# State columns by DMA, three PSUM banks for one image, and a pool placed last, in a four-layer network

## The chip, the cores and the metric

The kernel runs on one core of a Trainium2 chip, as one program for a whole four-layer network. The metric is the device time of that program in microseconds, the median of several runs; lower is better. A core has five instruction streams that matter here: TensorE (PE, matrix products and transposes into the PSUM banks), VectorE (DVE), ScalarE (ACT), GpSimd (POOL), and SyncE (SP), which in this kernel does nothing but issue DMA transfers, in order, each after its own waits.

## The reference

Four images of 64 x 64 positions with 128 channels (`x` of shape (4, 64, 64, 128), float32) pass four layers. Each layer computes `x + L(gn(x))`, where `gn` is a group norm with 32 groups and `L` is what the comment names.

```python
# layer 0: selective scan over the 4096 positions, in 4 directions, 256 channels, 16 states
def step(h, xs):
    ut, dt, bt, ct = xs
    dA = jnp.exp(dt[..., None] * A)
    h = dA * h + (dt * ut)[..., None] * bt[:, :, None, :]
    y = jnp.einsum('bkdn,bkn->bkd', h, ct)
    return (h, y)
# layer 1: spectral mixing along both axes, then a two-layer feed-forward part and a layer norm
# layer 2: attention between channels (tokens), with spectral convolutions, then a mixer
# layer 3: attention of each position over its 7 x 7 neighbourhood, 4 heads:
#   q, k, v = qkv(x);  softmax(q k / sqrt(32) + rpb) v;  proj;  + x
```

The scan is the heart of layer 0: each of 256 channels x 16 states carries its own `h` along the sequence, for each image and each of the 4 directions, so `h` at the end of one piece of the sequence starts the next piece.

## The kernel before

**Layer 0.** The sequence of 4096 positions is cut into 8 chunks of 512 (`NCH`, `CH`). A unit is one image, one direction `k` and one chunk `c`: 4 x 4 x 8 = 128 units, run one after the other. A unit has 16 slots, one for each state index `n`. In a slot GpSimd forms `dB` from `du` and one row of `Bb` (L485, 128 x 1024); ScalarE forms `dA`, the exponential, for the two halves of the channels (L491, 128 x 512 each); VectorE runs two scans (L492) that write `h` and start from a column of `state`. TensorE transposes the `h` of an earlier slot (`pt`, L379, seven slots behind), ScalarE copies the result out of PSUM (`hT`, L389), and TensorE multiplies it with `W` (L414) to sum over the states. Four slots make a group `g`, with one `h` tile (three buffers), one `Bb` and one `W`, both loaded by DMA. The order on each of the four engines is the order in which the code is written (`manual_schedule`); SyncE's order is left to the tile scheduler.

Other work is threaded into the slots: the input parts of the next unit (`inputs`: `xd`, `Ct`, `delta`, `du`), and for other images the convolution ahead of the scan (`before`) and the norm and projection behind it (`after`). A function `later(place, f, ..., slots=m)` puts an instruction into a list for a place in a slot `m` slots on ("act1" is behind the second `dA` of that slot), and `flush` (L446) issues it there. Line 446 is therefore the line of all deferred instructions in the profile.

`state` is a tile of 128 x 2 x 16 numbers. At the end of each group (`q == 3`), for all chunks of a direction but the last, the last column of the four states is copied from `h` to `state`, where the next chunk's scans read it. Before the change it is an instruction of ScalarE:

```python
later("act1", nc.scalar.copy, state[:, :, 4 * g : 4 * g + 4], h[:, :, CH - 1, :], slots=5)
```

This happens 4 images x 4 directions x 7 chunks x 4 groups = 448 times.

**Layers 2 and 3.** On-chip arrays are held in pools, placed one behind the other, and a layer's pools are given up at its end; an array of the next layer that lies at an address of an old one waits for the old one's last use. Layer 2 (`layer2_image`, reached through a pacing helper, so nearly all of its instructions have L883) opens `l2big`, `l2tmp` and `l2small` in this order; its result is stored from an array of the pool `big` (`x<-m`, four stores an image). Layer 3 opens its weight pool `l3w` first (L1423), so in before it begins at the address of `l2big`.

In layer 3 a generator `front(b)` prepares image `b`. It loads `x`, then runs three stages over eight chunks of 512 positions: transposes `pg` (L1454), whose statistics VectorE takes (L1455) and which ScalarE copies to `xn` (L1456); products `pv`, to which VectorE adds the bias in `vt` (two buffers), stored to DRAM by two DMAs a chunk; products `pk` (L1482), which ScalarE copies with a bias to `kp` (L1485). `queries` then forms `pq` for a row of blocks and loads `V`. All of `pg`, `pv`, `pk` and `pq` are tiles of `psM`, which has one PSUM bank. For image 0 `front` runs alone before any attention; for images 1 to 3 its steps are threaded into the attention of the image before. The attention scores `ps3` are in `psS`: two buffers of two banks each.

Of the kernel before, what the change touches and what calls it, by code (L numbers as in the profile page):

```python
# [2 lines left out]

# [7 lines left out]
F32 = mybir.dt.float32  # L11
# [71 lines left out]
def layer0(sh, A, x_in, x_out, scr):  # L83
# [7 lines left out]
    with ExitStack() as ctx:  # L91
# [352 lines left out]
        def later(place, f, *a, slots=1, **kw):  # L444

            todo.setdefault((slot + slots, place), []).append(lambda: f(*a, **kw))  # L446
# [10 lines left out]
        with tc.manual_schedule(engines=order):  # L457
            for i, (b, k, c) in enumerate(units):
# [14 lines left out]
                for n in range(NS):  # L473
                    slot = NS * i + n
                    g, q = divmod(n, 4)
                    if q == 0:
                        B_now = Bb
                        if g < 3:
                            Bb = broadcast(bd, g + 1)
                        elif i + 1 < len(units):  # L480
                            Bb = broadcast(bd_next, 0)
                        h = tmp.tile([P, 2, CH, 4], F32, name="h", bufs=3)
                        G = dict(unit=unit, g=g, h=h, q=0)
                    dB = tmp.tile([P, 2, CH], F32, name="dB", bufs=3)
                    nc.gpsimd.tensor_tensor(dB, du, B_now[:, q : q + 1, :].to_broadcast([P, 2, CH]), ALU.mult)  # L485
                    flush("dve")
                    if i + 1 < len(units) and n in (9, 11):
                        next(coming)
                    for s in range(2):
                        dA = psx.tile([P, CH], F32, name="dA", tag="x")  # L490
                        nc.scalar.activation(dA, delta[:, s, :], AF.Exp, scale=A_neg[:, k, s, n : n + 1])  # L491
                        nc.vector.tensor_tensor_scan(  # L492
                            h[:, s, :, q], dA, dB[:, s, :], state[:, s, n : n + 1], ALU.mult, ALU.add
                        )
                        if s == 0 and i + 1 < len(units):
                            if n in (7, 8, 10):
                                next(coming)
                        elif n == 7 and i + 1 < len(units):
                            bd_next, Wd_next = next(coming)
                        flush(f"act{s}")  # L500
                    copy = transposed() if slot >= LAG else (lambda: None)
                    copy()
                    flush("act2")
                    if q == 2:
                        W = Ws[g] = tmp.tile([P, 32, 16], F32, name="W", bufs=4)
                        nc.sync.dma_start(W, Wd[g, 0 : P * CH].rearrange("(p t a) -> p t a", p=P, a=16))
                    if q == 3:
                        queue.append(G)
                        if c < NCH - 1:
                            later("act1", nc.scalar.copy, state[:, :, 4 * g : 4 * g + 4], h[:, :, CH - 1, :], slots=5)  # L510

                    if i + 1 < len(units):
                        if n == 1:
                            u_next, v_next = fetch(*units[i + 1])
                        if n == 6:
                            coming = inputs(*units[i + 1][1:], v_next, (i + 1) % 2)
                        if n in (6, 7, 9):
                            next(coming)
                        if n == 13:
                            ready = next(coming)  # L520

                    if n == 10:
                        y = unit["y"] = tmp.tile([P, 4, 2 * P], F32, name="y", tag="t4", bufs=4)
                        if k == 0:
                            src = scr("y3").rearrange("(w q r) d -> r w q d", w=64, r=2)
                            for r in range(2):
                                nc.sync.dma_start(y[64 * r : 64 * r + 64], src[r, :, 4 * c : 4 * c + 4, :])
                        elif k != 1:
                            nc.sync.dma_start(y, dst(1 if k == 3 else 0))

                    inside = [d for d in sides if d.inside]
                    free = n not in BUSY and not inside and slot >= taken
                    able = dict(f=False, l=False, m=free, n=free and n != 5, z=free and n != 5, c=free and n == 11)
                    for d in inside or [d for d in sides if able[d.need] and d.due(slot)][:1]:
                        taken = slot + dict(m=1, n=2, z=2, c=3)[d.need]
                        d.free_at = slot + 1
                        d.step()
                    for d in sides:
                        if d.need in ("f", "l") and d.due(slot):
                            if d.need == "l":  # L540
                                d.free_at = slot + 3
                            d.step()
                    sides = [d for d in sides if d.need]
# [833 lines left out]
def layer2(sh, w, wp, x_in, x_out, scr, wt):  # L1377
    tc, nc = sh.tc, sh.nc
    with ExitStack() as ctx:
        pool = lambda name, bufs, **kw: ctx.enter_context(tc.tile_pool(name=name, bufs=bufs, **kw))  # L1380
        ps = pool("l2ps", 3, space=PSUM)
        for name, shape in (("XG", [64, 5, P]), ("BD", [P, P])):
            w[name] = [wp.tile(shape, F32, name=f"{name}{n}") for n in range(2)]
            for t in w[name]:
                nc.vector.memset(t, 0.0)
        for t in w["XG"]:
            nc.vector.memset(t[:, 4, 64:65], 1.0)
        pools = pool("l2big", 1), pool("l2tmp", 1), pool("l2small", 1), ps
        paced = copy(sh)
        paced.nc = Pace(nc)  # L1390
        engines = {mybir.EngineType.PE, mybir.EngineType.Activation, mybir.EngineType.DVE, mybir.EngineType.Pool}
        free = [0, 1]
        pairs = [[] for _ in range(NB // 2)]

        def image(b):
            n = free.pop(0)
            yield from layer2_image(paced, w, pools, x_in(b), x_out(b), (scr(n), scr(2 + n)), wt, n, pairs[b // 2])
            free.append(n)

        with tc.manual_schedule(engines=engines):  # L1400
            paced.nc.in_turn((image(b) for b in range(NB)), 2)


def layer3(sh, A, x_in, out, v_pads):
# [5 lines left out]
    with ExitStack() as ctx:  # L1410
# [31 lines left out]

        def front(b):

            x = big.tile([P, NJ, DM], F32, name="x3")
            load_image(nc, x, x_in(b))
            xn = big.tile([P, NT], F32, name="xn3")
# [1 line left out]
            yield  # L1449
            st = small.tile([P, NCH, 6], F32, name="gn_st", bufs=2)  # L1450
            for c in range(NCH):
                pg = psM.tile([P, CH], F32, name="pg3", tag="m")
                for q in range(4):
                    nc.tensor.transpose(pg[:, q * P : (q + 1) * P], x[:, 4 * c + q, :], sh.ident)  # L1454
                nc.vector.bn_stats(st[:, c, :], pg)  # L1455
                nc.scalar.copy(xn[:, c * CH : (c + 1) * CH], pg)  # L1456
                yield
# [4 lines left out]
                nc.vector.tensor_scalar(xc, xc, s_, o_, ALU.mult, ALU.add)  # L1462
            yield
            for c in range(NCH):
                pv = psM.tile([P, 4, P], F32, name="pv3", tag="m")
                for q in range(4):
                    nc.tensor.matmul(
                        pv[:, q, :],
                        lhsT=xn[:, (4 * c + q) * P : (4 * c + q + 1) * P],
                        rhs=w["qkv"][:, 2 * P : 3 * P],  # L1470
                        start=True,
                        stop=True,
                    )
                vt = tmp.tile([P, 4, P], F32, name="vt")
                tt(vt, pv, w["v_b"].unsqueeze(1).to_broadcast([P, 4, P]), ALU.add)
                rows = v_pads[b % 2][3 + 8 * c : 11 + 8 * c, 3:67, :].rearrange("(q r) c d -> r c q d", r=2)
                for r in range(2):
                    nc.sync.dma_start(rows[r], vt[64 * r : 64 * r + 64])
                yield
            for c in range(NCH):  # L1480
                pk = psM.tile([P, CH], F32, name="pk3", tag="m")
                nc.tensor.matmul(  # L1482
                    pk, lhsT=w["qkv"][:, P : 2 * P], rhs=xn[:, c * CH : (c + 1) * CH], start=True, stop=True
                )
                nc.scalar.activation(  # L1485
                    kps[b % 2][:, 3 + 8 * c : 11 + 8 * c, 3:67],
                    pk.rearrange("p (h w) -> p h w", w=64),
                    AF.Identity,
                    bias=w["qkv_b"][:, 1:2],
                )  # L1490
                yield
# [343 lines left out]
```

## Time and profile before

The time is 8299.07 us, the median of 3 runs (8296.89 to 8299.89). The profiled execution has a span of 8299.4 us.

| engine | busy us | share of the span | instructions |
|---|---|---|---|
| PE matmul | 6571.5 | 79% | 52976 |
| DVE | 6753.8 | 81% | 7948 |
| ACT | 6229.0 | 75% | 10246 |
| POOL | 5482.7 | 66% | 2502 |
| DMA, SyncE's queue | | 44.0% of 16 engines | 1279618 packets |

Busy time doesn't include waits, and matmul ends are modelled. The shares are means over four layers with different limits: layer 0 ends at about 6006 us, layer 1 lies between that and about 6636, layer 2 goes on to 7692, and layer 3 takes the rest. A row of a group gives busy time, mean nanoseconds of one instruction and the idle time of its engine just before it, with what ended most of that. An arrow `a<-b` reads "a is made from b", and `[0.92 <-ACT dA L491]` in a timeline says that the engine stood idle 0.92 us until that instruction of another engine let it go.

### The profile page before, as it was taken

Reading aid. Unit: us, or ns where it says so; the run is one execution under the profiler, and the core shown is the slowest. Engines: PE = TensorE matmul, PEld = TensorE weight load, DVE = VectorE, ACT = ScalarE, POOL = GpSimd, SP = SyncE. Lnnn points to the kernel's source line nnn. Section 1 sums busy time; section 2 is a strip of 40 time slices with the busy share of each in tenths; the row PEclk is TensorE's granted clock in tenths of the full one; section 3 lists DMA queues with packets and bytes.
Section 4 is the critical chain, followed back from the end, with each engine's and each line's share of the span. In section 5 each row is a group of like instructions: output and inputs, shape, how many; then the busy total and the mean of one; then the engine's idle time right before and its main releaser. Section 6 shows DMA issues by size and latency. Waiting matters only on the chain.

```text
span 8299.4 us, 140501 instructions
## 1 busy us (share of the span) xinstructions
PE 6571.5 (79%) x52976; PEld 4171.0 (50%) x52976; DVE 6753.8 (81%) x7948; ACT 6229.0 (75%) x10246; POOL 5482.7 (66%) x2502
## 2 busy tenths in 40 slices
PE   7788888778788877888877777787779878686689
PEld 3444454444445444444544444454467766464456
DVE  2889999998999999889999999999944545645578
ACT  3899999989899898989988999999822213315467
POOL 0889889988888898888889999999800011020233
PEclk9899999999999999999999999999989988788799
DMA  6445555445555544455555445455442041331332
GB/s 127 153 143 188 162 164 176 158 156 166 176 168 172 173 165 161 157 169 168 176 179 170 157 156 185 174 174 181 148 103 43 23 118 35 87 101 31 96 94 79
DMA packets 1281977, 1163.78 MB, mean 140 GB/s; under 512 B 637973, under 2 KB 1075825, under 8 KB 1214354
## 3 DMA queue, kind: packets, MB, share of 16 engines
q1 hardware_dynamic: 1279618, 1153.06, 44.0%
q8 instruction: 417, 6.83, 0.3%
q14 instruction: 262, 2.15, 0.1%
q10 hardware_dynamic: 1680, 1.74, 0.1%
HBM read 962.66 MB, written 189.74 MB: 139 GB/s over the span
## 4 chain that ended last, share of the span: by engine, by line
PE 21%; ACT 11%; DVE 11%; issue 3%; DMA 2%; POOL 2%; SPq 1%; DVEq 0%; ACTq 0%; POOLq 0%
DVE h L492 4%; ACT hT L389 4%; ACT dA L491 4%; PE pt L379 2%; PE po L695 1%; PE pf L690 1%; POOL dB L485 1%; PE pz L883 1%; PE pu L883 1%; PE pt L1518 1%; DVE in_st L883 1%; PE pb L883 1%; DVE m L883 1%; PE pa L883 1%; PE ps L1572 1%
## 5 line engine op out<-in xcount | busy, mean ns | idle before, releaser
L492 DVE TENSOR_TENSOR_SCAN h<-dA,state,dB 128x512 f32<-128x512 f32 x4096 | 4958.8, 1269 | 361.5 <-ACT dA L491 247.2
L485 POOL TENSOR_TENSOR dB<-du,Bb 128x1024 f32<-128x1024 f32 x2048 | 4817.0, 2385 | 550.7 <-DVE h L492 381.9
L379 PE MATMUL pt<-ident,h 128*128 128x128 f32 x16384 | 2249.0, 281 | 1014.9 <-ACT hT L389 1010.0
L379 PEld LDWEIGHTS pt<-ident,h 128*128 128x128 f32 x16384 | 1838.5, 143 | 2051.6 <-ACT hT L389 1806.4
L491 ACT ACTIVATE dA<-delta,A_neg 128x512 f32<-128x512 f32 x4096 | 2746.1, 690 | 163.8 <-DVE h L492 140.8
L389 ACT COPY hT<-pt 128x1024 f32<-128x1024 f32 x2048 | 2068.3, 1010 | 176.9 <-PE pt L379 163.4
L414 PE MATMUL yT<-hT,W 128*32 128x256 f32 x16384 | 1396.9, 414 | 2.7 <-DVE y L430 2.1
L883 POOL COPY XG<-Xs 64x9 f32<-64x9 f32 (+2 forms) x44 | 10.9, 292 | 1020.8 <-ACT Xs L883 1020.7
L414 PEld LDWEIGHTS yT<-hT,W 128*32 128x32 f32 x16384 | 454.4, 150 | 352.0 <-issue 336.9
L214 PE MATMUL cv<-xn,taps 128*128 128x512 f32 x1152 | 612.8, 632 | 0.0
L1556 POOL TENSOR_TENSOR S<-S,sm 128x784 f32<-128x784 f32 x128 | 191.1, 1493 | 403.1 <-DVE sm L1554 251.9
L325 PE MATMUL dp<-xd,w_dt 65*128 65x512 f32 x512 | 298.1, 665 | 103.9 <-ACT Ct L312 91.8
L334 POOL TENSOR_TENSOR du<-delta,u 128x1024 f32<-128x1024 f32 x128 | 305.1, 2383 | 67.6 <-DVE delta L331 67.6
L214 PEld LDWEIGHTS cv<-xn,taps 128*128 128x128 f32 x1152 | 183.4, 188 | 234.0 <-issue 232.6
L306 PE MATMUL xd_ps<-u,w_x 128*48 128x512 f32 x512 | 251.8, 615 | 40.9 <-DMA u<-l_xw 16.8
L1563 ACT ACTIVATE S<-S,mx 128x196 f32<-128x196 f32 x512 | 227.9, 448 | 33.0 <-DVE mx L1590 32.4
L691 ACT ACTIVATE h<-pf,b 128x512 f32<-128x512 f32 x128 | 88.0, 687 | 146.7 <-PE pf L690 146.7
L331 DVE SCALAR_TENSOR_TENSOR delta<-delta,dp 128x512 f32<-128x512 f32 x256 | 169.2, 661 | 25.7 <-ACT delta L329 25.7
L325 PEld LDWEIGHTS dp<-xd,w_dt 65*128 65x128 f32 x512 | 79.4, 195 | 219.5 <-ACT Ct L312 150.4
L1432 POOL MEMSET kp<- 128x210 f32 (+1 forms) x8 | 1.8, 286 | 275.0 <-DMA x<-m 275.0
L328 ACT ACTIVATE delta<-dp 128x512 f32<-128x512 f32 x256 | 152.4, 595 | 28.4 <-PE dp L325 23.8
L329 ACT ACTIVATE delta<-delta 128x512 f32<-128x512 f32 x256 | 162.3, 634 | 8.1
(335 smaller groups left out, 7183.8 us busy)
## 6 DMA issues: line engine op xcount, KB each, us to landing
Bb<-l_B SPq DMA_DIRECT2D x512, 1024.0 KB
W<-l_W SPq DMA_DIRECT2D x512, 256.0 KB
l_y<-y SPq DMA_DIRECT2D x128, 512.0 KB
u<-l_xw SPq DMA_DIRECT2D x64, 512.0 KB
y<-l_y SPq DMA_DIRECT2D x64, 512.0 KB
u<-l_xr SPq DMA_DIRECT2D x64, 512.0 KB
V<-l_v SPq DMA_DIRECT2D x512, 49.0 KB
wr<-wt SPq DMA_DIRECT2D x128, 136.0 KB
```

The lines of the kernel that those rows point to most:

```text
L214: nc.tensor.matmul(pm, lhsT=taps[:, s, t, :], rhs=xn[:, dy : dy + 8, dx : dx + 64], start=(t == 0), stop=(t == 8),)
L306: nc.tensor.matmul(xd_ps, lhsT=w_x[:, s, k, :], rhs=u[:, s, :], start=(s == 0), stop=(s == 1))
L325: nc.tensor.matmul(dp, lhsT=w_dt[:, k, s * P : (s + 1) * P], rhs=xd, start=True, stop=True)
L334: nc.gpsimd.tensor_tensor(du, delta, u, ALU.mult)
L379: nc.tensor.transpose(pt[:, j, s, :], G["h"][:, s, t0 : t0 + 32, :].rearrange("p t n -> p (t n)"), sh.ident)
L389: return lambda: nc.scalar.copy(hT, pt.rearrange("p j s d -> p j (s d)"))
L414: nc.tensor.matmul(U["yT"][e][32 * jo : 32 * jo + 32, qo % 2, :], lhsT=U["Ws"][G["g"]][:, :, 4 * q + j], rhs=hT[:, j, :], start=((e, jo) n ...
L485: nc.gpsimd.tensor_tensor(dB, du, B_now[:, q : q + 1, :].to_broadcast([P, 2, CH]), ALU.mult)
L491: nc.scalar.activation(dA, delta[:, s, :], AF.Exp, scale=A_neg[:, k, s, n : n + 1])
L492: nc.vector.tensor_tensor_scan(h[:, s, :, q], dA, dB[:, s, :], state[:, s, n : n + 1], ALU.mult, ALU.add)
L883: r = f(*args, **kw)
L1563: nc.scalar.activation(Sn, Sn, AF.Exp, bias=U["mx"][:, n : n + 1], accum_out=sm[:, n : n + 1])
```

## The change

Three edits. The state columns go from `h` to `state` by a DMA that SyncE issues, written at the end of the group itself and not five slots later. The pool `l2big` is opened after `l2tmp` and `l2small`, so that layer 3's first arrays lie where these two were and not where the arrays are from which layer 2 stores its last result. And for image 0 of layer 3 `front` takes its PSUM tiles in turn from `psM` and from the two buffers of the scores, three banks in all. Lines of the changed kernel are one to ten higher than those of before.

```diff
-                            later("act1", nc.scalar.copy, state[:, :, 4 * g : 4 * g + 4], h[:, :, CH - 1, :], slots=5)
+                            nc.sync.dma_start(state[:, :, 4 * g : 4 * g + 4], h[:, :, CH - 1, :])
...
-        pools = pool("l2big", 1), pool("l2tmp", 1), pool("l2small", 1), ps
+        tmp, small, big = pool("l2tmp", 1), pool("l2small", 1), pool("l2big", 1)
+        pools = big, tmp, small, ps
...
         def front(b):
 
+            ring = itertools.count()
+
+            def bank(name):
+                if b == 0 and next(ring) % 3:
+                    return psS.tile([P, 2, CH], F32, name="ps3")[:, 0, :]
+                return psM.tile([P, CH], F32, name=name, tag="m")
...
-                pg = psM.tile([P, CH], F32, name="pg3", tag="m")
+                pg = bank("pg3")
...
-                pv = psM.tile([P, 4, P], F32, name="pv3", tag="m")
+                pv = bank("pv3").rearrange("p (q d) -> p q d", q=4)
...
-                pk = psM.tile([P, CH], F32, name="pk3", tag="m")
+                pk = bank("pk3")
```

More of the change, by code (lines that the diff above doesn't have):

```diff
@@ L1 @@
+import itertools
 from contextlib import ExitStack
```

## The prediction

> **What bounds the kernel now.** I read the page first: busy time, slices and dearest groups.
>
> ```profile
> DVE  2889999998999999889999999999944545645578
> PEclk9899999999999999999999999999989988788799
> L492 DVE TENSOR_TENSOR_SCAN h<-dA,state,dB 128x512 f32<-128x512 f32 x4096 | 4958.8, 1269 | 361.5 <-ACT dA L491 247.2
> ```
>
> A slice is 207 us. VectorE is at 80 to 90% through the first three quarters, layer 0, and one group, the scan, does three fifths of the span. The clock row falls only in the last quarter.
>
> Second, the busy time of each engine between 216 and 6006 us, layer 0's steady loop (columns: length; busy PE, PE weight load, DVE, ACT, POOL; clock; DMA share; GB/s), and VectorE's largest waits there (sum, count, longest):
>
> ```profile
> 216.00:6006.00 5790.00, 4606.56 (x36113) 2729.94 (x36114) 5401.90 (x5127) 5265.52 (x7879) 5183.43 (x2252) 0.98 0.51 167
> DVE h L492 <- ACT dA L491: 247.2, 406, 1.9
> DVE h L492 <- POOL dB L485: 90.9, 51, 4.9
> ```
>
> DVE, ACT and POOL are busy 93, 91 and 90%. They are near balance, so relieving one of them is worth only the part of its work on which the others wait. VectorE stands still 5790 - 5402 = 388 us (about 372 us in the scan's slots), 247 of it for ScalarE's `dA`.
>
> Third, the state copies, as their own row of groups by shape and once in the timeline (columns: start, length):
>
> ```profile
> L446 ACT COPY state<-h 128x8 f32<-128x8 f32 x448 | 82.6, 184 | 0.0
> ```
> ```profile
> 2507.45 0.18 ACT L446 COPY state<-h 128x8 f32<-128x8 f32 x1
> 2507.54 0.63 ACT L446 ACTIVATE e<-e 128x512 f32<-128x512 f32 x1
> 2508.07 0.99 ACT L389 COPY hT<-pt 128x1024 f32<-128x1024 f32 x1
> 2508.96 0.70 ACT L491 ACTIVATE dA<-delta,A_neg 128x512 f32<-128x512 f32 x1
> 2509.76 2.46 DVE L492 TENSOR_TENSOR_SCAN h<-dA,state,dB 128x512 f32<-128x512 f32 x2 [0.92 <-ACT dA L491]
> ```
>
> The copy never waits (0.0 in the last column); it only takes room. Here it stands in an unbroken ScalarE chain at whose end VectorE had stood 0.92 us: in such a slot its 0.18 us is on the path.
>
> Fourth, the seam of layers 2 and 3, where image 0's `front` runs alone. Timeline, then windows:
>
> ```profile
> 7692.36 0.35 SPq L1423 DMA_DIRECT2D qkv<-in_qkv_w  x1
> 7699.87 10.21 SPq L720 DMA_DIRECT2D x<-x  x8
> 7704.34 1.09 PE L1454 MATMUL pg<-ident,x 128*128 128x128 f32 x4 [32.63 <-DMA x<-x]
> 7705.53 0.70 DVE L1455 BATCH_NORM_STATS2 gn_st<-pg 128x6 f32<-128x512 f32 x1 [10.48 <-PE pg L1454]
> 7706.31 0.58 ACT L1456 COPY xn<-pg 128x512 f32<-128x512 f32 x1 [20.42 <-DVE gn_st L1455]
> 7706.95 1.12 PE L1454 MATMUL pg<-ident,x 128*128 128x128 f32 x4 [1.52 <-ACT xn L1456]
> ```
> ```profile
> 7704.34:7724.60 20.26, 8.89 (x32) 5.69 (x32) 5.96 (x9) 4.68 (x8) 0.00 (x0) 0.50 0.55 166
> 7728.70:7751.60 22.90, 16.58 (x64) 14.26 (x64) 6.70 (x9) 0.00 (x0) 0.00 (x0) 0.50 0.36 94
> 7751.60:7774.50 22.90, 16.61 (x17) 4.02 (x17) 0.00 (x0) 5.55 (x8) 0.00 (x0) 0.50 0.25 70
> 6813.20:6823.50 10.30, 10.24 (x31) 4.90 (x31) 0.00 (x0) 5.47 (x8) 0.00 (x0) 0.76 0.78 182
> 6644.50:6651.70 7.20, 5.43 (x32) 4.85 (x32) 5.19 (x9) 0.00 (x0) 0.00 (x0) 0.79 1.15 290
> ```
>
> PE, DVE and ACT go strictly in turn, since the next `pg` needs the bank that the ACT copy has just read; PE runs at half clock. The three windows are `pg`, `pv` and `pk`, 66 us with almost nothing beside them. The last two windows are layer 2's likenesses of `pk` and `pg`, with several banks: 10.3 against 22.9 us, and 7.2 against 20.3.
>
> **What the Trainium skill says.** "PSUM — Partial Sum Buffer", section "PSUM bank collisions raise a hardware error": two engines must not be on one bank at once, readers included. The trace agrees: ACT's `xn` copy, which needs only `pg`, starts after the statistics end. "TensorE: Matmul & The Clock Gate", section "Part 1: The HAM clock gate": the array starts at half rate and warms only when kept busy for some microseconds. The trace agrees: 0.50 through the front, 0.76 where layer 2 keeps PE busy. "DMA: Bandwidth & Descriptors", section "Anatomy of one DMA — SWDGE (gpsimd) path": about 2 us fixed for a transfer, mostly the receipt; here the first 512 KB of `x` took about 4.4 us, so I take 2 to 4 us for 4 KB of states; no row of before shows one. Its section "Why small descriptors are slow (HBM only)" says that small packets between SBUF and SBUF don't suffer as those of HBM do; no run so far shows one.
>
> **Part 1, states by DMA.** 448 copies leave ScalarE (4 images x 4 directions x 7 chunks x 4 groups), 448 x 0.184 = 82.6 us. Not all is on the path. Taking each copy in the trace, in 185 cases ScalarE ran without a gap from the copy to a wait of VectorE (90 in slot 8 of 16, 50 in slot 4, 23 in slot 12, 22 elsewhere); in the other 263 ScalarE idled first, as it does most in slot 6. That is 185 x 0.184 = 34 us. I take 28, as a slot won here is partly lost at the next wait for GpSimd (91 us of those remain). Ends: 0, if the next wait takes it all; 82.6, if ScalarE were the bound throughout.
>
> What it adds: SyncE issues 448 transfers. The nearest row, the `Ct` writes with their many small pieces, takes a median of 0.36 us: 160 us of issue over 5790, on a queue that has these waits alone:
>
> ```profile
> SPq L340 <- POOL dB L485: 1960.7, 324, 14.0
> ```
>
> So the issue is hidden. The added wait is SyncE's, for the last scan of a group. Behind it queue `Bb`, `W`, `u` and the next unit's small loads. In the changed order each `Bb` load that follows a state transfer belongs to a group at least three groups on and waits for GpSimd anyway; the tightest, the next unit's second group, is left about 17 us, against 2 to 4 for a state plus about 6 for a 1 MB `Bb`. Whoever reads the state is the next chunk's scan, 12 slots or more away: 12 x 2.83 = 34 us. `h` is reused 8 slots (22.6 us) after its end; today the copy comes only 5 slots after. Packets: 448 x 256 = 114,688 of 16 bytes. At the mean of all of before (44% x 16 x 8299 / 1,279,618 = 46 ns) they take 5.2 ms, 328 us of each of 16 engines, 0.51 to 0.57 of the loop at most: no bound. Part 1: -28.
>
> **Part 2, pool order.** With the arrays placed last, layer 3's weights no longer wait for layer 2's last `x<-m` stores. In the changed order fourteen loads stand before these stores, so layer 3's `x` goes at about 7692.4 instead of 7699.87: -7.5. The weights wait for `tmp`'s last use instead, near 7624, hidden under the last layer-2 image. At layer 2's start the `xg` loads go directly behind the last store, ahead of `wr`, whose issue held them from 6636.51 to 6639.10: -2.6.
>
> **Part 3, three banks.** `pg`: layer 2's likeness needed 12.6 us from the issue of the load to the end of its statistics; here it was 7724.6 - 7692.4 = 32.2 less a little, 31.6 with the same end marks. So 31.6 - 12.5 = -19.1, which includes the 7.5 above. `pv`: eight steps of 2.86 us. The PE time, 16.6, stays at half clock; `vt` has two buffers, so step n waits for the landing of n-2: addition 0.69, two issues 1.24, about 2 landing, some 4 us for two steps at best. With V stores between, I take 2.3 a step, 18.5: -4.4 (ends 16.6 and 19.2). `pk`: 22.9 to 10.3 as in layer 2 if the clock warms: I take 12, -10.9; the cold end is 16.6, -6.3. The first `pq`: -0.5. Images 1 to 3 keep one bank and run under attention, where PE is full: 0. Sum of the seam: -19.1 - 4.4 - 10.9 - 0.5 = -34.9.
>
> **Sum.** -28 - 2.6 - 34.9 = -65.5: 8299.1 - 65.5 = 8233.6, say 8233.
>
> **The rivals.** *A: the sum*, 8233. *B: layer 0 gains nothing.* For it: POOL is busy 90% and scans wait 91 us for it; against it: 185 copies stand right before a wait for `dA`. Seam alone, -38: 8261. *C: slower.* The state transfers hold up what is queued behind them on SyncE, or small pieces slow the big loads. For it: DMA share is 0.51, and `Bb` and `W` are in the same queue; against it: `Bb` has 17 us. At 0.25 us of stall for each of 448, +112, less 38 at the two seams and 28 in the scans: 8299 + 112 - 66 = 8345 (8373 without the 28). *D: ScalarE is the bound throughout.* For it: 247 of 388 us idle wait on it; against it: it idles 114 us in slot 6. -82.6 - 38: 8178.
>
> **How the numbers follow.** A 0.66, B 0.17, C 0.08, D 0.07, and 0.02 for a seam worth only 20 with layer 0 as it is (8279). Range 8195 to 8270: the low end is 60 us from scans with a seam of 44 at its best; the high end is B with a cold `pk` and slow `pv`. Faster by over 0.2% (16.6 us) is A, B, D and most of the last: 0.90; within, 0.03; slower, C's 0.07.
>
> **What would show it.** Right: no `state<-h` on ScalarE, 448 more issues on SyncE's queue; in the loop ScalarE about 83 less, VectorE's wait for `dA` 25 to 35 less, no scan waiting on a DMA; the loop's end some 28 us earlier; the `x` of layer 3 issued within a microsecond of the last store; `pg` about 8 us, `pk` at 1.3 to 2 a step. Wrong: scans waiting on DMA `state` or `dB` waiting on DMA `Bb` for more than the copy's 0.18 (then C), or `dA` waits that fall while waits on `dB` rise by as much (B), or `pv` held by its stores at 2.9 a step.

## The result and the profile after

The changed kernel took 8235.44 us (median of four runs; 8233.59 to 8247.49) against 8299.48 us before (also four): a ratio of 0.9925, with a 95% interval of 0.9908 to 0.9943. The profiled executions, 8299.4 and 8232.3 us, can be split at the same points. "First S" is the first addition of the bias to the scores in layer 3.

| stretch | before | after | difference |
|---|---|---|---|
| start to first scan | 225.5 | 225.6 | +0.1 |
| first to last scan (layer 0's loop) | 5781.2 | 5755.1 | -26.1 |
| last scan to layer 2's first `pg` | 637.8 | 634.7 | -3.1 |
| from there to layer 2's last store issued | 1044.9 | 1046.2 | +1.3 |
| to the issue of layer 3's `x` | 10.4 | 3.0 | -7.4 |
| issue of `x` to first S | 79.2 | 43.4 | -35.8 |
| first S to the end | 520.4 | 524.3 | +3.9 |

First the page of the changed kernel: slices, the scan's group, and SyncE's DMA queue (packets, MB, share of 16 engines).

```profile
DVE  2889999998999999889999999999944554635778
PEclk9899999999999999999999999999989989798799
L493 DVE TENSOR_TENSOR_SCAN h<-dA,state,dB 128x512 f32<-128x512 f32 x4096 | 4960.2, 1271 | 340.3 <-ACT dA L492 211.7
q1 hardware_dynamic: 1401474, 1154.93, 45.5%
```

The scan is as busy as before (4960 us); what shrank is the idle time ahead of it, 361.5 to 340.3, most of it in waits for `dA`, so the gain is mainly in ScalarE's lateness. Next, the busy time in the loop (same columns as before), VectorE's waits and SyncE's:

```profile
216.00:5980.00 5764.00, 4600.03 (x36114) 2727.96 (x36115) 5400.60 (x5127) 5228.49 (x7431) 5183.04 (x2252) 0.98 0.52 168
```
```profile
DVE h L493 <- ACT dA L492: 211.7, 366, 2.1
DVE h L493 <- POOL dB L486: 85.7, 48, 4.9
DVE h L493 <- issue: 18.1, 40, 1.4
DVE h L493 <- DMA W<-l_W: 7.4, 5, 1.5
```
```profile
SPq L511 <- DVE h L493: 1109.8, 290, 11.5
SPq L341 <- POOL dB L486: 1096.1, 273, 12.8
```

ScalarE has 448 instructions fewer, but its busy time in the loop fell by 37.0 us (5265.5 to 5228.5), not by the 83 that the prediction gave as a sign: 37.0 / 448 = 0.083 us a copy. The reason is that ScalarE's instructions overlap in the trace. The timeline in the prediction shows it: the copy starts at 2507.45 and is recorded as 0.18 us long, but the next instruction starts at 2507.54, only 0.09 us later. The median of all 448 copies in before is 0.088 us from start to next start.

SyncE's waits mostly changed their name: where it stood 1960.7 us for `dB`, it now stands 1109.8 us for the end of a group and 1096.1 us for `dB`. Scans wait 85.7 us for `dB`, not more than the 90.9 of before, so `Bb` isn't late. VectorE's waits for `dA` changed their names too. "Issue" rose from 5.4 to 18.1 us, and five waits stand under the load of `W`, which a scan doesn't read. In these five, and in 37 of the 40 under "issue", the scan started 0.09 us after its `dA` had ended, so they are waits for `dA`. Counted that way (waits over 0.15 us whose scan starts within 0.13 us of the end of its `dA`), before has 251.2 us and after 235.2. The waits for `dA` fell by 16.0 us, not by the 35.5 that the names suggest, and the trace shows no scan that waited for a DMA.

The transfer itself, from the view of its line (duration min/median/max in ns):

```profile
L511 SPq DMA_DIRECT2D state<-h x448: 599/600/1944, 235.1 to 5935.0; - x150
```

From the start of its issue to the end of its last packet such a transfer took 2.05 us (median, worked out from the packets).

Then the seam: SyncE's queue and the engines in the timeline, and the stages by window (`pg`; group scale; `pv`; `pk` to first scores).

```profile
7664.63 9.96 SPq L721 DMA_DIRECT2D x<-x  x8
7668.81 1.08 PE L1463 MATMUL pg<-ident,x 128*128 128x128 f32 x4 [24.96 <-DMA x<-x]
...
7683.34 2.76 SPq L1487 DMA_DIRECT2D l_v<-vt  x4
7686.44 1.70 SPq L1520 DMA_DIRECT2D V<-l_v  x2
7688.24 2.62 SPq L1487 DMA_DIRECT2D l_v<-vt  x4
...
7692.65 0.69 DVE L1484 TENSOR_TENSOR vt<-pv,v_b 128x512 f32<-128x512 f32 x1 [3.95 <-DMA l_v<-vt]
...
7707.11 1.58 PE L1581 MATMUL ps<-kp,q 32*64 32x196 f32 x32 [0.87 <-ACT q L1509]
```
```profile
7668.81:7676.22 7.41, 6.45 (x32) 5.50 (x32) 5.41 (x8) 4.10 (x7) 0.00 (x0) 0.68 1.15 347
7676.22:7680.51 4.29, 0.94 (x5) 0.80 (x5) 2.64 (x8) 0.85 (x2) 0.00 (x0) 0.59 0.61 185
7680.51:7694.71 14.20, 9.91 (x64) 9.34 (x65) 5.32 (x7) 0.00 (x0) 0.00 (x0) 0.86 0.35 90
7694.71:7707.11 12.40, 10.75 (x20) 3.93 (x19) 1.38 (x2) 6.38 (x10) 0.00 (x0) 0.75 0.45 120
```

`pg` takes 7.4 us where it took 20.3, and the clock column, 0.50 throughout before, is 0.86 in `pv`. What now holds `pv` stands in the last column of the `vt` line: VectorE waits for the store of an earlier `vt`, and the stores share SyncE's queue with the first `V` loads, whose issue holds the queue for 1.6 to 1.7 us at a time. Before, VectorE waited at `vt` for the products alone. Its waits there, before and after:

```profile
DVE vt L1475 <- PE pv L1467: 16.2, 8, 2.2
```
```profile
DVE vt L1484 <- DMA l_v<-vt: 9.6, 5, 3.9
```

### The profile page after: what moved, and what is told of

It is laid out like the page before. It is cut to its first block, busy times and chain, and to the rows that moved or that the text cites. A ratio compares the mean times of both kernels' runs of the same rounds, so it can differ in the third digit from the quotient of the medians.

```text
span 8232.3 us, 141196 instructions
## 1 busy us (share of the span) xinstructions
PE 6551.1 (80%) x52976; PEld 4166.6 (51%) x52976; DVE 6752.2 (82%) x7948; ACT 6192.0 (75%) x9798; POOL 5481.8 (67%) x2502
## 3 DMA queue, kind: packets, MB, share of 16 engines
q1 hardware_dynamic: 1401474, 1154.93, 45.5%
## 4 chain that ended last, share of the span: by engine, by line
PE 21%; DVE 11%; ACT 10%; issue 3%; DMA 2%; POOL 2%; SPq 1%; ACTq 0%; DVEq 0%; POOLq 0%
DVE h L493 5%; ACT hT L390 4%; ACT dA L492 3%; PE pt L380 2%; POOL dB L486 1%; PE po L696 1%; PE pf L691 1%; PE pz L884 1%; PE pt L1527 1%; PE pu L884 1%; DVE in_st L884 1%; PE pb L884 1%; DVE m L884 1%; PE pa L884 1%; PE ps L1581 1%
## 5 line engine op out<-in xcount | busy, mean ns | idle before, releaser
L493 DVE TENSOR_TENSOR_SCAN h<-dA,state,dB 128x512 f32<-128x512 f32 x4096 | 4960.2, 1271 | 340.3 <-ACT dA L492 211.7
L884 POOL COPY XG<-Xs 64x9 f32<-64x9 f32 (+2 forms) x44 | 10.9, 293 | 1016.6 <-ACT Xs L884 1016.5
L1527 PE MATMUL pt<-ident,S 128*98 128x128 f32 x1024 | 165.3, 286 | 3.3 <-POOL S L1565 1.9
```

What stands on the lines that cost most here:

```text
L493: nc.vector.tensor_tensor_scan(h[:, s, :, q], dA, dB[:, s, :], state[:, s, n : n + 1], ALU.mult, ALU.add)
L884: r = f(*args, **kw)
L1527: nc.tensor.transpose(pt[:, half, hp, :], U["S"][:, e, hp, 98 * half : 98 * half + 98], sh.ident)
```

## The experiments

**Each part alone.** `states_only` is before with the one line of the transfer; `pools_only` and `banks_only` are before with the other two edits one at a time; `seams_only` has both and ScalarE's copies:

```diff
-                            nc.sync.dma_start(state[:, :, 4 * g : 4 * g + 4], h[:, :, CH - 1, :])
+                            later("act1", nc.scalar.copy, state[:, :, 4 * g : 4 * g + 4], h[:, :, CH - 1, :], slots=5)
```

> Before, with the state columns by DMA alone. Theory 1 (the parts are independent, the scan loop gains what the changed kernel's loop gained): the last scan ends about 26 us earlier, time 8299 - 26 = 8273, all of it in layer 0. Rival (part of the loop's gain in the changed kernel was chance, or the transfers cost more than they look): within 10 us of before.

> The changed kernel with ScalarE's deferred copies put back: pool order and three banks alone. Theory 1: layer 0 as before (within 5 us), the start of layer 2 about 2 us shorter, the seam before layer 3 about 42 us shorter, of which up to 4 may be lost again in the attention by a lower granted clock: 8299 - 41 = 8258. Rival: the attention gives nothing back, 8255 or less.

> Before, with the pool order alone. Theory 1: weights are loaded ahead of the last stores, so x of layer 3 is issued about 7.5 us earlier, and layer 2 starts 2 us earlier: -9.5, 8290; the stages pg, pv and pk keep their 20, 23 and 23 us. Rival (the earlier load only meets the same wait for the bank or for the last store): no gain, 8297 to 8301.

> Before, with the three banks alone. Theory 1: x comes as late as before, the three stages shrink from about 70 us to about 38: -32, 8267. Rival (the stages gain only together with the earlier loads, because pg is then bound by the arrival of x): -20, 8279.

| kernel | median us | ratio to before | loop us | last store to `x` | `x` to first S | first S to end |
|---|---|---|---|---|---|---|
| states_only | 8282.38 | 0.9975 (0.9966 to 0.9985) | 5748.2 | 10.2 | 79.1 | 526.0 |
| seams_only | 8258.90 | 0.9946 (0.9929 to 0.9962) | 5787.3 | 3.0 | 43.3 | 525.0 |
| pools_only | 8292.85 | 0.9988 (0.9981 to 0.9995) | 5770.9 | 3.0 | 78.8 | 523.7 |
| banks_only | 8273.64 | 0.9964 (0.9951 to 0.9977) | 5783.2 | 10.6 | 43.0 | 528.9 |

Within these intervals the parts are independent: pool order (0.12%) and banks (0.36%) agree with the 0.54% of both, and with the states' 0.25% with the 0.75% of the whole. In the stretches of the table each edit shows at its own place. The time from the last scan to layer 2's last store, which the table leaves out, is 1682.7 us in before, 1674.7 in pools_only and 1692.9 in states_only, so single profiles don't add up as the medians do. Two more numbers are less exact than they look. The loop of kernels with the same layer 0 differs by up to 16 us (5770.9 to 5787.3; mean with before 5780.7). And the attention takes 520.4 us in before and 523.7 to 528.9 in the four others, with pools_only among them, so the +3.9 of the table isn't something that three banks cause.

**Is it the engine or the place?** ScalarE keeps the copies, in other slots:

```diff
-                            nc.sync.dma_start(state[:, :, 4 * g : 4 * g + 4], h[:, :, CH - 1, :])
+                            later("act1", nc.scalar.copy, state[:, :, 4 * g : 4 * g + 4], h[:, :, CH - 1, :], slots=(3, 5, 2, 2)[g])
```

> The changed kernel with the state copies on ScalarE again, but put 3, 5, 2 and 2 slots after the ends of the four groups (slots 6, 12, 13 and 1 of a unit, where ScalarE has the most idle time) in place of 5 each (slots 8, 12, 0, 4). Theory 1 (a copy costs only where VectorE then waits for a late dA; the changed kernel won half of its loop gain in slot 10, behind the copy of slot 8): the loop wins 13 to 26 of the 29 us without any DMA, about 8240. Rival 1 (ScalarE is in order and each copy costs the same wherever it stands): as with the two seams alone, 8258. Rival 2 (two or three slots after a group ScalarE must wait for the group's last scan, and is then late for the next dA): slower than 8258.

8231.18 us, ratio 0.9914 (0.9900 to 0.9928): as much as by DMA. ScalarE does all of its copies, as the row of groups says,

```profile
L447 ACT COPY state<-h 128x8 f32<-128x8 f32 x448 | 83.3, 186 | 0.0
```

and they cost next to nothing. Then only the first group's copy was moved, `slots=(3, 5, 5, 5)[g]`:

> The changed kernel with the state copies on ScalarE, of which only the first group's is moved, from slot 8 to slot 6; the other three stay 5 slots after their groups. Theory 1 (half of the loop's gain is in slot 10, behind the copy of slot 8): VectorE's idle time in slot 10 falls from 49 to about 38 us and the loop wins 12 to 15 us over the two seams alone, 8244. Rival (the gain is spread over the four copies evenly): a quarter, 7 us, 8251, with slot 10 hardly changed.

8248.99 us, ratio 0.9926 (0.9914 to 0.9939), 0.20% below the two seams alone, though the two intervals overlap; the loop is 5765.0, 16 us below the mean of 5780.7. One copy of four seems to carry half of the gain or more; as loops with one layer 0 differ by 16 us, one trace can't say it more exactly.

**What does the transfer cost?** None at all (then every chunk starts from the zero state, so the carried part of the scan is left out), and two instead of one:

```diff
-                        if c < NCH - 1:
-                            nc.sync.dma_start(state[:, :, 4 * g : 4 * g + 4], h[:, :, CH - 1, :])
```
```diff
+                            nc.sync.dma_start(spare_state[:, :, 4 * g : 4 * g + 4], h[:, :, CH - 1, :])
```

> The changed kernel without any copy of the state columns: every chunk's scans start from the zero state, so the carried part of the scan is left out; the work of each engine is else the same. Theory 1 (the transfers are hidden): as the changed kernel, 8235, within 5 us. Rival (the transfers cost on SyncE's queue or in the DMA engines): faster than the changed kernel by more than 10 us, 8225 or less.

> The changed kernel with a second transfer of each state column, to a spare tile: 448 more transfers of 256 pieces. Theory 1 (SyncE and the DMA engines have room): as the changed kernel, 8235, within 5 us. Rival (each transfer costs): slower by what a transfer costs times 448; 0.05 us each would give 22 us, 8257.

8234.72 us (0.9914, 0.9900 to 0.9927) without and 8229.24 us (0.9906, 0.9891 to 0.9921) with twice as many, against 8235.44. The transfers are hidden; no cost can be measured. VectorE's waits of the kernel without copies, in the same window as above, bear this out:

```profile
DVE h L493 <- ACT dA L492: 222.5, 397, 1.9
DVE h L493 <- POOL dB L486: 92.0, 50, 4.9
DVE h L493 <- issue: 3.5, 5, 1.4
```

318.0 us in sum, against 211.7 + 85.7 + 18.1 + 7.4 = 322.9 with the transfers.

**Two copies on ScalarE** (the two seams, and behind each copy a second one, to a spare tile):

> The changed kernel with ScalarE's deferred copies put back and a second copy of each column, to a spare tile, right behind. Theory 1 (about a third of a copy's 0.18 us is on the path, as in the removal): 448 x 0.065 = 29 us more than the two seams alone, 8287. Rival 1 (ScalarE bounds the loop throughout): 83 more, 8341. Rival 2 (the room is used up slowly, the removed copies were only late ones): within 8 us of 8258.

8300.06 us, ratio 0.9994 (0.9986 to 1.0002), 0.48% or 40 us over the two seams alone; in the profile the loop is 5823.1, 42 us over the mean of 5780.7. So 448 copies more cost 42 us (0.094 us each), and 448 fewer won 26 (0.058 each): dearer than expected when added. ScalarE's busy time in the whole run rose by 41.1 us (6229.9 to 6271.0), so the added copies cost about all the time that they took of ScalarE; the 83 us of their recorded lengths were never there to lose. That ScalarE isn't the bound throughout is shown by the copies in other slots: there it is as busy (6227.0 us), and the loop is 25 us shorter than with the two seams alone (5762.6 against 5787.3).

The next table is worked out from the traces: VectorE's idle time in two of the 16 slots, summed over all units, and how many of 128 units have a slot 10 of over 4 us (start of its first scan to the start of the next slot's; mean 4.5 to 4.8, against about 3.2 in the others).

```
                 loop us   idle in slot 4   idle in slot 10   units with a long slot 10
copies_twice     5823.1    47.2             71.6              28
seams_only       5787.3    41.9             49.3              15
before           5781.2    41.1             47.0              14
copy0_placed     5765.0    42.5             39.0              12
copies_placed    5762.6    37.7             38.1              11
after            5755.1    37.2             36.7               8
states_none      5749.7    36.7             27.5               4
states_twice     5745.1    37.2             29.3               4
```

Moving the first group's copy changes slot 10 and leaves slot 4 (42.5); moving the others mends slot 4. What a copy costs in a typical unit is seen in the median length of slot 10: 3.425 us with two copies ahead of it (copies_twice), 3.340 with one (before) and 3.257 with none (after), 0.08 us for each. Part of slot 10's cost comes in lumps: a unit is either short or 1.2 to 1.6 us longer. One long case, in the kernel with two copies, in the timeline and by windows:

```profile
2265.79 2.08 PE L326 MATMUL dp<-xd,w_dt 65*128 65x512 f32 x2
2267.90 0.60 ACT L329 ACTIVATE delta<-dp 128x512 f32<-128x512 f32 x1 [1.42 <-PE dp L326]
2268.53 0.63 ACT L330 ACTIVATE delta<-delta 128x512 f32<-128x512 f32 x1
2269.07 0.68 ACT L493 ACTIVATE dA<-delta,A_neg 128x512 f32<-128x512 f32 x1
2269.78 1.29 DVE L494 TENSOR_TENSOR_SCAN h<-dA,state,dB 128x512 f32<-128x512 f32 x1 [1.76 <-ACT dA L493]
```
```profile
2260.00:2263.75 3.75, 1.97 (x18) 1.08 (x17) 2.90 (x3) 3.72 (x9) 2.38 (x1) 1.00 0.76 54
2263.75:2268.00 4.25, 4.25 (x20) 2.14 (x21) 4.25 (x5) 2.83 (x5) 3.40 (x2) 0.63 0.88 212
```

Read upwards: the scan waits for `dA`, this stood in line behind the two activations of `delta`, these waited for `dp`, and `dp` took 2.08 us at a clock of 0.63, after a stretch in which TensorE was busy 1.97 of 3.75 us. In all long units of five traces (before, after, seams_only, states_none, copies_twice) `dp` took 1.4 to 2.1 us; its mean in the short ones is 1.13 to 1.16. In the record of the granted clock, which in the loop is either 1 or 0.5, `dp` met the 0.5 in every long unit, and in a short one only four times, all in copies_twice. Was the clock let down because TensorE idled? Sixteen products with a zero tile were put into the two gaps, on top of four `vt` buffers (the edit that is described last):

```diff
+            for n in range(2):
+                for j in range(4):
+                    nc.tensor.matmul(
+                        U["yT"][qo // 2][32 * j : 32 * j + 32, qo % 2, :],
+                        lhsT=idle,
+                        rhs=hT[:, j, :],
+                        start=False,
+                        stop=False,
+                        skip_group_check=True,
+                    )
...
-                    copy = transposed() if slot >= LAG else (lambda: None)
+                    copy = transposed(n in (7, 8)) if slot >= LAG else (lambda: None)
```

> The changed kernel with four buffers of vt and, in slots 7 and 8 of every unit, eight products more of a zero tile with hT, added to the same sums (0.67 us of TensorE each time, where it stood idle 1.3 and 1.8 us). In every trace so far 4 to 28 of 128 units have a slot 10 of 4.6 us in place of 3.2, and in each of these units the dp products run at a lowered clock (1.4 to 2.1 us in place of 1.1). Theory (the clock falls where TensorE has had too little to do in slots 7 and 8; late copies lengthen that idle time, so a part of a copy's price is this): 0 to 3 such units in place of 10, the loop 8 to 14 us shorter than with four buffers alone (5761), about 5749. Rival 1 (the clock falls for the power that is drawn, or by chance): as many such units as before, 4 to 10 or more. Rival 2 (the products delay pt or dp): the loop is longer than 5761.

8653.96 us, ratio 1.0413 (1.0399 to 1.0427): a miss, by an added wait. The products of slot 7 belong to the last part of the unit before, whose sums VectorE is just then adding to `y`; the fillers had to wait for that, and `dp` behind them:

```profile
2358.70 1.93 PE L403 MATMUL yT<-hT,idle 128*32 128x256 f32 x16 [2.60 <-DVE y L450]
2360.57 2.08 PE L326 MATMUL dp<-xd,w_dt 65*128 65x512 f32 x2
2362.74 0.60 ACT L329 ACTIVATE delta<-dp 128x512 f32<-128x512 f32 x1 [3.75 <-PE dp L326]
```

VectorE's idle time in slot 8 went from 35 us (with four buffers alone) to 380. No unit had a long slot 10 any more. A unit has two `dp` stages: the second, ahead of slot 10, met the half clock in none of 127 units, against 10 with four buffers alone, while the first, behind the new wait, met it in 85, against 2. The clock fell less often where TensorE was given work and more often where it was made to stand, though everything in these slots had moved as well.

The clock record of the other traces says more. All its changes in the loop lie on one grid of steps of 3.413 us. In the changed kernel each of the 39 falls followed a step in which TensorE was busy 63% of the time or less (by products whose ends are modelled; 46% on average, 81% in the steps of full clock that no fall followed), and in 35 of them no single gap of TensorE was longer than 3 us. With the fillers there were 103 falls, against 36 with four buffers alone, all behind such steps. So idling goes ahead of every fall, and several short gaps are enough for it. That it is the whole cause isn't shown: 285 of the 1582 other steps had as little work and no fall behind them.

**The stores of `vt`.** One argument, `bufs=4` on the tile `vt`, on the changed kernel; with it SyncE's order changes too, and all sixteen stores of `front` come ahead of the first `V` loads.

```diff
-                vt = tmp.tile([P, 4, P], F32, name="vt")
+                vt = tmp.tile([P, 4, P], F32, name="vt", bufs=4)
```

> The changed kernel with four buffers of vt in place of two (the sixteen V stores are then queued in one row, ahead of the first V loads). Theory 1 (with three banks the pv stage is bound by the landing of the V stores: VectorE stood 9.6 us for them in the changed kernel's trace): from the issue of x to the first scores 38 us in place of 43.4, the whole 5 us faster than the changed kernel, 8230. Rival (TensorE at half clock, 16.6 us, is as long as the stores): no change, 43.

8217.84 us, ratio 0.9890 (0.9875 to 0.9905), below both kernels. From the issue of `x` to the first S it took 35.9 us instead of 43.4, and SyncE's queue shows the stores in one row:

```profile
7694.25 12.48 SPq L1487 DMA_DIRECT2D l_v<-vt  x16
7706.78 5.57 SPq L1520 DMA_DIRECT2D V<-l_v  x7
```

VectorE's wait for them at this seam is all but gone:

```profile
DVE vt L1484 <- DMA l_v<-vt: 0.3, 1, 0.3
```

Whether the buffers alone or the new order of the queue did this, the run doesn't separate.

The attention, too, is shorter: 516.5 us, and 516.4 and 516.7 in the two other kernels with four buffers, against 520.4 to 528.9 in all with two. That was not expected. VectorE's waits ahead of `vt` in the attention fell from 17.5 to 11.5 us, which may be a part of it; its cause stays open.

> Both together without any state transfer: copies on ScalarE 3, 5, 2 and 2 slots after the groups, and four buffers of vt. Theory 1: as the changed kernel with four buffers, within 5 us, about 8230. Rival (the idle slots hold the copies only in part): 5 to 10 us slower than that.

8216.37 us, ratio 0.9894 (0.9880 to 0.9907): without any state transfer, the same.

## Why the prediction was right, and where it wasn't

The forecast was 8233 by way of -28 in the loop, -2.6 at layer 2's start and -34.9 at the seam. The runs bear out where the gain is, the likeliest case; layer 0 without gain, a delay by the transfers, and ScalarE as the bound throughout are out. That the sum fits so closely is in part luck: the profiles show -26.1, -3.1 and -7.4 - 35.8 = -43.2, and what the seam gave beyond the forecast, 8 us, was about made up for by less in the loop (1.9 us), by layer 2 (+1.3) and by the attention (+3.9), which vary by as much without any of the edits.

**States by DMA, -28.** The profile shows -26.1; three kernels with one transfer each (after, states_only, vt_four: 5755.1, 5748.2, 5760.7) lie 26 us below the four with ScalarE's copies five slots on. By the medians of states_only it is 0.25%, 12 to 28 us. The wait was the right one, VectorE's for `dA`, but the number came near in part by luck, because the price of a copy was mis-sized. I took its recorded length, 0.184 us. A copy overlaps its neighbours and takes 0.083 us of ScalarE's busy time, and 0.08 us of slot 10 in a typical unit. The 185 cases at 0.088 us from start to next start give 16 us (an estimate), and the waits for `dA` fell by 16.0. The remaining 10 us of the loop lie in smaller waits, in which single profiles differ anyway; the forecast had none of them and took 6 us off. For the same reason the upper end of this term, ScalarE's full price of 82.6 us, should have been 37.

That only copies in an unbroken chain of ScalarE ending in a wait of VectorE count, held up: it put 90 of 185 such copies in slot 8, moving that copy alone won about 16 of the 26 us, and slots in which ScalarE idles took all four copies at no cost that can be measured. It showed more: since only the place counts, the DMA wasn't needed. What the reading lacked as well is that a late `dA` isn't only worth its own delay: part comes as lumps of 1.2 to 1.6 us in slot 10, which may be why a copy was worth 0.058 us when taken away and 0.094 when added.

**The transfers, hidden.** Right, and shown by none and two. The 2 to 4 us taken for one transfer fit the 2.05 us of the trace. Two terms were mis-sized without effect: the issue takes 0.60 us, not 0.36, so 448 x 0.60 = 269 us of SyncE and not 160; and the 328 us of each DMA engine were 64 (last section).

**Pool order, -7.5 and -2.6.** The stretch to the issue of `x` fell by 7.4, layer 2's start by 3.1; the latter is less sure, as that stretch takes 632.7 to 638.9 us in the kernels with the new order and 637.1 to 641.8 in those without. Of the remaining 3.0 us SyncE stood 2.7 for the landing of the last store.

**`pg`, -19.1.** From the issue of `x` to the end of the statistics it was 24.1 us and is 11.6: -12.5. (The prediction's 31.6 counts from 7692.4, where `x` was to go.) With the 7.4 of the pool order, which the term includes, that is -19.9. Layer 2's likeness was the right model.

**`pv`, `pk`, `pq`, -4.4 - 10.9 - 0.5 = -15.8.** Measured from the first `pv` to the first scores: 48.7 to 26.6, -22.1. This is the term that was mis-sized most. I held `pv` to the half clock, 16.6 us of TensorE, and added the two stages one behind the other. In fact the clock rose in `pv` as well (9.9 us for its 64 products), and `pk` began while VectorE still stood for the stores of `vt`. The rule in the Trainium skill, "TensorE: Matmul & The Clock Gate", "Part 1: The HAM clock gate", that an array kept busy warms up, which I had applied to `pk` alone, held for `pv` too (0.86). That the stores bind `pv` was right: VectorE stood 9.6 us for them, and four buffers took 7.5 us off.

**Images 1 to 3, 0.** Within what kernels with the same attention differ by.

One slip is in the chances: A, B and D alone make 0.90, so with most of the last case it is about 0.92 for faster, and "slower" has 0.07 where C has 0.08.

## What to carry to other kernels

An instruction on a busy engine costs only where the next engine then waits, so price it, in an unbroken chain, from its start to the next start and not by its recorded length; and before it is handed to another engine, try to put it into a slot where its own engine idles: here that alone was worth as much as a DMA. When a stage loses one bound, read at once which wait ends last now; here three banks uncovered two buffers, and one argument more was worth 7.5 us at this seam. And look at the order that a scheduler gives a queue: here loads stood between stores for which a buffer waited, and held the queue for 1.6 us or more at a time.

## What the runs showed of the hardware

TensorE's clock fell inside a loop in which its mean was 0.98: in 4 to 28 of 128 units, at the same place, `dp` took up to 2.08 us instead of 1.1. The Trainium skill, "TensorE: Matmul & The Clock Gate", section "Part 1: The HAM clock gate", says that the window over which activity is judged runs freely, so that the moment of a change differs between runs of one kernel. The traces agree: the changes of the clock lie on a grid of 3.413 us that doesn't follow the loop's units of some 45 us, and kernels with the same layer 0 had 10, 12, 14 and 15 such units. Their loops took 5771 to 5787 us; the long units account for about 6 of these 16 us.

The 114,688 packets of 16 bytes that carry the states took 8.9 ns each (worked out from the packets), 1018 us in all or 64 us of each of 16 engines; the mean of all packets in before is 46 ns. The whole queue went from 44.0% of 16 x 8299 us to 45.5% of 16 x 8232, about 1500 us more, but the other packets, too, took longer in that run. The Trainium skill, "DMA: Bandwidth & Descriptors", section "Why small descriptors are slow (HBM only)", says that packets between SBUF and SBUF don't suffer from being small. No run here shows that: there are no packets of this size on another route, and by bytes these are slow, 1.8 bytes per ns on an engine against 23 for the packets of 8192 bytes.
